# Side work of an attention-and-scan kernel: results taken one step later, with a third PSUM bank

## Chip, cores and metric

One core of a Trainium2 chip. The metric is the time on the device in microseconds (us); of several runs the median counts.

## What is computed

The input x holds 16 images of 256 channels by 1024 positions, in fp32. Two layers follow each other, each added to x:

- Layer 0: a group norm (16 groups), then a transformer block: layer norm, attention with four heads of 32 over the 1024 positions, projection, a second layer norm, a feed-forward pair of matrices with GELU.
- Layer 1: a second group norm, then a state-space layer. From the normed input come u and z (512 channels each), a gate, and from u the step sizes (softplus), B and C (64 states each). The heart is a recurrence along the 1024 positions:

```python
def step(h, inp):
    d_t, B_t, C_t, u_t = inp
    dA = jnp.exp(d_t[..., None] * A)
    h = dA * h + (d_t * u_t)[..., None] * B_t[:, None, :]
    y = jnp.einsum('bdn,bn->bd', h, C_t)
    return (h, y)
...
y = (ys + u * D) * silu(z)
out = (y @ out_proj_w.T) * sigmoid(gate)
```

It runs over 512 channels with 64 states each, so over 32768 rows of 1024 positions per image.

## The kernel before

**The main loop.** The recurrence is cut into units: one unit is 2 x 128 rows by 512 positions, so an image has 256 units and the run 4096. The list `units` (line 805) goes over image b, half t of the positions, channel block k, quarter q and i from 0 to 7. For each unit n the loop (lines 946 to 984) issues, in this order:

- `load(n + 6)`: SP loads a 512 KB tile dub (line 832), and at times the tiles bt, ct and pieces;
- `inputs(n + 4)`: POOL multiplies it with B (line 842);
- `scan(n, 0)` and `scan(n, 1)`: DVE runs the two recurrences (line 864);
- `decay(n + 2)`: PE makes the exponents (line 851) and ACT the exponentials (line 854), in four PSUM banks (pool `aps`), which come free with the scans;
- a piece of side work, if one is due;
- pieces of `outputs` (line 888): PE multiplies with C (lines 901 and 913), ACT copies out, SP stores ys. It takes a group of eight units at once, and its pieces on PE lie in the units i = 0 to 5 of the next group.

**The side work.** While image b is scanned, everything else is done beside it: `first_norm(b + 1)`, `gate_and_store(b - 1)`, `attention_layer(b + 1)` and `scan_inputs(b + 1)`, in this order (line 952). They are generators. Each `yield` gives a weight, and the loop takes the next step when enough has come due:

```python
rate, due = total / (UNITS - AHEAD - 3), 0.0
...
due += rate
while due > 0.0:
    due -= next(side, 1e9)
```

A step of weight 1 is thus about one unit, and two small steps can fall in the same unit. For image 0 the side work runs ahead of the loop, where nothing else runs; the last `gate_and_store` runs behind it.

**Order.** Lines 995 to 1005 hold PE, ACT, DVE and POOL to the order in which the code issues the instructions. SP's order is chosen by the scheduler. Each engine works through its own queue in order, so an instruction that waits holds up all behind it.

**PSUM.** There are eight banks: four of `aps`, one of `yps` (outputs), one of `accp` (the attention's sum of values, tag "av") and two of `mm`. In the loop all results of the side work are in the two banks of `mm` in turn, by `psum` (line 98).

**The places that the change touches:**

- `group_norm` (line 225): sums on DVE, means on PE (line 233), variance through Ln and Exp on ACT (lines 258, 259), then the multiplication on DVE (line 262). It runs in `first_norm` (tile gn) and in `scan_inputs` (tile xp).
- `layer_norm` (line 266): per half of the positions a mean on PE (line 270, ln_m), the subtraction on DVE (line 277), squares on ACT (line 279), the variance on PE (ln_v), Ln and Exp on ACT (lines 294, 296), the multiplication on DVE (line 301). It runs twice in `attention_layer`.
- z in `scan_inputs` (lines 567 to 588): eight products on PE (line 580), each with a tanh on ACT (line 585). `finish_z` multiplies on DVE (line 569) and stores (line 571) at the next step.
- Softplus (lines 684 to 736), for four channel blocks d: `begin` (PE, then absolute value and Exp on ACT), `more` (copy and relu on ACT, lines 694, 695), `rest` (two subtractions on DVE, lines 699, 700), then Ln and three splittings.
- Output product in `gate_and_store` (lines 783 to 799): four results in eight steps on PE (line 789); `finish` takes each on DVE (lines 776, 778) after the next product's first half. `come` holds loads that are issued step by step (line 309: ys, ud, zs, gs, xr, kept), before DVE uses them (lines 760, 764).
- `spread_c` (line 873): once per image POOL clears cd, a tile of 128 x 4096 (line 876), and for each half of the positions ACT writes C into a few of its places with eight copies (line 880).

Of the kernel before, what the change touches and what calls it, by code (L numbers as in the profile page):

```python
# [11 lines left out]
F32 = mybir.dt.float32  # L12
# [7 lines left out]
P = 128  # L20
# [3 lines left out]
HL = 512  # L24
# [9 lines left out]
TB = 512  # L34
# [18 lines left out]
def attention_then_scan_kernel(  # L53
# [44 lines left out]
    def psum(name, dims=P):  # L98
        src = mm if beside["scan"] else next(alone)
        return src.tile([P, HL], F32, name=name, tag="mm" if src is mm else "a")[:dims]  # L100

    def work(name, n=L):
        return wide.tile([P, L + 2 + CONV], F32, name=name, tag="wide")[:, :n]
# [4 lines left out]
    def hs(h):  # L108
        return ts(h, HL)
# [71 lines left out]
    for k in range(KC):  # L181
# [5 lines left out]
        nc.sync.dma_start(rel[ts(k, P), :], t)  # L187


    def weights(*specs):  # L190
# [34 lines left out]
    def group_norm(src, dst):  # L225
# [33 lines left out]
        nc.scalar.activation(v, v, AF.Exp, scale=-0.5)  # L259
        yield 1.5  # L260
        for k in range(KC):
# [4 lines left out]
    def layer_norm(src, dst, g, b):  # L266
        def mean_of(parts, name):
            m = psum(name)
            for k in range(KC):
                nc.tensor.matmul(m, avg, parts[k], start=(k == 0), stop=(k == KC - 1))  # L270
            return m
# [10 lines left out]

        m = mean_of([t[:, hs(0)] for t in src], "ln_m")
        yield 1
        q0 = centre(0, m)
        m = mean_of([t[:, hs(1)] for t in src], "ln_m")
        yield 1.2
        q1 = centre(1, m)
        vs = [mean_of(q0, "ln_v")]
        yield 1.2  # L290
        vs.append(mean_of(q1, "ln_v"))
        yield 1
        for v in vs:
            nc.scalar.activation(v, v, AF.Ln, bias=eps)
        for v in vs:
            nc.scalar.activation(v, v, AF.Exp, scale=-0.5)
        yield 2
        for h in range(2):
# [238 lines left out]
    def scan_inputs(b):  # L537
# [28 lines left out]

        def finish_z():
            for d, hf, z, t, ps in ready:
                nc.vector.scalar_tensor_tensor(z[:, hs(hf)], t, 1.0, ps, ALU.add, ALU.mult)
                if hf == 1:  # L570
                    nc.sync.dma_start(zs[ts(d, P), :], z)
            ready.clear()

        for d in range(ND):
            z = work("z")
            for hf in range(2):
                finish_z()
                ps = psum("z_ps")
                for k in range(KC):
# [124 lines left out]
        for d in range(ND):  # L704
            items = [more(d, *items[0]), begin(d, 1)]
            yield 1
            items[1] = more(d, *items[1])
            rest(*items[0])
            yield 1.4
            rest(*items[1])  # L710
# [32 lines left out]
    def gate_and_store(b):  # L743
# [39 lines left out]
        for o in range(KC):  # L783
            for hf in range(2):
                ps = psum("m_ps")
                for q in range(2):
                    first = o * HL + hf * 2 + q
                    for d in range(ND):
# [3 lines left out]
                        )  # L792
                    if q == 0:
                        finish()
# [77 lines left out]

    def spread_c(b, t):
        if t == 0:
            now["cd"] = hst.tile([P, TB // 16, P], F32, name="cd", tag="cd")
            nc.gpsimd.memset(now["cd"], 0.0)
        ct = blocks[b, t]["ct"].rearrange("p (a c e) -> p a c e", c=4, e=4)
        for c in range(4):
            for j in range(2):
                nc.scalar.activation(  # L880
                    now["cd"][:, :, 40 * c + j : 40 * c + j + 7 : 2], ct[:, :, c],
                    AF.Identity, scale=par[:, j : j + 1],
                )
# [4 lines left out]
    def outputs(b, t, k, q):  # L888
        if (k, q) == (0, 0):
            now["yb"] = yps.tile([P, HL], F32, name="yb", tag="yb")  # L890
            nc.vector.memset(now["yb"][:, 256:], 0.0)  # L891
        cd, yb, hbuf = now["cd"], now["yb"], now["h", q % 2]
        out4 = yb[:, 256:].rearrange("p (j a m e) -> p a e j m", a=2, j=2, e=4)
# [52 lines left out]
    for n, (b, t, k, q, i) in enumerate(units):  # L946
# [32 lines left out]
        if i == 0 and n > 0:  # L979
            g = outputs(*units[n - 1][:4])  # L980
            next(g)
            running.append(g)
        if (k, q, i) == (0, 0, 6):
            spread_c(b, t)
    for g in running:
# [75 lines left out]
```

## Time and profile before

| What | us |
|---|---|
| Median of three runs | 13823.3 (13804.61 to 13835.7) |
| Profiled execution, its own time | 13784.86 |
| Span of the profiled execution | 13782.7 |
| of it before the first scan | 392.8 |
| of it behind the last scan | 45.3 |
| VectorE busy | 12135.5 (88%) |
| TensorE busy | 11113.2 (81%) |
| GpSimd busy | 10477.2 (76%) |
| ScalarE busy | 8088.7 (59%) |
| Mean granted TensorE clock | 0.732 of full speed |

PE, DVE, ACT, POOL and SP are TensorE, VectorE, ScalarE, GpSimd and SyncE. A row of the costliest groups names line, engine, operation and tiles, how often it ran, then its busy time and the mean of one in ns, and behind the bar how long the engine stood idle just before and what ended that. The table of waits says the same per pair: who waited, for whom, how long in all, how often, and the longest. "issue" is idle time for which the profile shows no cause.

### The profile page before, as it was taken

Reading aid. Unit: us, or ns where it says so; the run is one execution under the profiler, and the core shown is the slowest. Engines: PE = TensorE matmul, PEld = TensorE weight load, DVE = VectorE, ACT = ScalarE, POOL = GpSimd, SP = SyncE. Lnnn points to the kernel's source line nnn. Section 1 sums busy time; section 2 is a strip of 40 time slices with the busy share of each in tenths; the row PEclk is TensorE's granted clock in tenths of the full one; section 3 lists DMA queues with packets and bytes.
Section 4 is the critical chain, followed back from the end, with each engine's and each line's share of the span. In section 5 each row is a group of like instructions: output and inputs, shape, how many; then the busy total and the mean of one; then the engine's idle time right before and its main releaser. Section 6 shows DMA issues by size and latency. Waiting matters only on the chain. (4 is left out here: it accounts for less than half of the span.)

```text
span 13782.7 us, 435036 instructions
## 1 busy us (share of the span) xinstructions
PE 11113.2 (81%) x185744; PEld 5728.7 (42%) x185744; DVE 12135.5 (88%) x11699; ACT 8088.7 (59%) x14245; POOL 10477.2 (76%) x8214
## 2 busy tenths in 40 slices
PE   7787878878787787978879788797887978878767
PEld 3344444444444444444444444444444444434434
DVE  3898898898898889888898888889888898888898
ACT  3666665656655565655656655566555655556644
POOL 0787777777787777777777787777777777777788
PEclk8686767867777686876767777677776776867767
DMA  1566566565665656556565565656656565565666
GB/s 55 196 207 230 187 214 208 201 222 196 211 207 199 218 201 223 194 199 218 197 231 186 197 226 191 232 185 202 219 191 230 187 214 205 194 228 187 209 219 223
DMA packets 964174, 2804.18 MB, mean 203 GB/s; under 512 B 138162, under 2 KB 285747, under 8 KB 962228
## 3 DMA queue, kind: packets, MB, share of 16 engines
q1 hardware_dynamic: 962228, 2776.34, 58.8%
q8 instruction: 1452, 23.79, 0.7%
q14 instruction: 494, 4.05, 0.1%
HBM read 2514.18 MB, written 261.62 MB: 201 GB/s over the span
## 5 line engine op out<-in xcount | busy, mean ns | idle before, releaser
L842 POOL TENSOR_TENSOR dub<-dub,bt 128x512 f32<-128x512 f32 x8192 | 10422.4, 1307 | 3254.5 <-DMA dub<-dus 2878.4
L854 ACT ACTIVATE a<-a,acol 128x512 f32<-128x512 f32 x8192 | 5064.9, 660 | 3728.2 <-PE a L851 3689.1
L864 DVE TENSOR_TENSOR_SCAN h<-a,last,dub 128x512 f32<-128x512 f32 x4096 | 4932.9, 1261 | 227.0 <-POOL dub L842 128.8
L864 DVE TENSOR_TENSOR_SCAN h<-a,dub 128x512 f32<-128x512 f32 x4096 | 4700.9, 1201 | 276.7 <-POOL dub L842 186.6
L851 PE MATMUL a<-pieces,pick 48*128 48x512 bf16 x8192 | 2914.9, 480 | 2103.1 <-DVE h L864 2037.8
L901 PEld LDWEIGHTS yb<-h,cd 128*32 128x32 f32 x131072 | 2677.2, 140 | 2166.2 <-issue 1847.3
L901 PE MATMUL yb<-h,cd 128*32 128x64 f32 x131072 | 3090.5, 265 | 160.9 <-DVE yb L891 115.9
L851 PEld LDWEIGHTS <-pick 48*128 48x128 bf16 x8192 | 498.0, 96 | 2507.4 <-issue 2293.2
L408 PE MATMUL s_ps<-ka,qa 32*128 32x512 f32 x2048 | 1115.7, 1009 | 23.2 <-DVE mx L399 15.2
L399 DVE TENSOR_REDUCE mx<-s_ps 128x1 f32<-128x512 f32 x1024 | 654.9, 678 | 279.0 <-PE s_ps L408 278.2
L913 PEld LDWEIGHTS yb<-turn,y 128*16 128x16 f32 x32768 | 418.9, 120 | 960.3 <-ACT y L909 484.6
L909 ACT COPY y<-yb 128x256 f32<-128x256 f32 x1024 | 383.4, 374 | 693.6 <-PE yb L901 688.3
L913 PE MATMUL yb<-turn,y 128*16 128x32 f32 x32768 | 555.2, 216 | 193.8 <-ACT y L909 173.0
L444 PE MATMUL st_ps<-qa,ka 33*128 33x512 f32 x2048 | 590.2, 613 | 25.9 <-ACT pt L452 25.5
L432 PE MATMUL av<-pt,vv 128*64 128x512 f32 x2048 | 572.7, 635 | 4.3 <-ACT sums L390 3.3
L452 ACT ACTIVATE pt<-st_ps 128x512 f32<-128x512 f32 x1024 | 558.9, 609 | 28.8 <-PE st_ps L444 28.4
L408 PEld LDWEIGHTS s_ps<-ka,qa 32*128 32x128 f32 x2048 | 345.4, 274 | 402.3 <-DVE mx L399 221.4
L630 PE MATMUL g_ps<-w,xp 128*128 128x256 f32 x1536 | 475.2, 468 | 0.0
L630 PEld LDWEIGHTS g_ps<-w,xp 128*128 128x128 f32 x1536 | 401.9, 329 | 137.6 <-issue 92.6
L789 PE MATMUL m_ps<-w,xs 128*128 128x256 f32 x1024 | 316.7, 459 | 10.9 <-DVE xs L764 10.9
L921 ACT COPY yo<-yb 128x256 f32<-128x256 f32 x512 | 193.1, 377 | 222.2 <-PE yb L913 219.7
L615 DVE SCALAR_TENSOR_TENSOR u<-up,cwh,u 128x1024 f32<-128x1024 f32 x192 | 300.9, 1567 | 23.8 <-ACT u L607 23.6
(135 smaller groups left out, 7593.8 us busy)
## 6 DMA issues: line engine op xcount, KB each, us to landing
dub<-dus SPq DMA_DIRECT2D x4096, 512.0 KB
dps<-pc SPq DMA_DIRECT2D x384, 128.0 KB
pieces<-dps SPq DMA_DIRECT2D x1024, 48.0 KB
xs<-in_x_dram SPq DMA_DIRECT2D x64, 512.0 KB
xs<-kept SPq DMA_DIRECT2D x64, 512.0 KB
zs<-z SPq DMA_DIRECT2D x64, 512.0 KB
ud<-u SPq DMA_DIRECT2D x64, 512.0 KB
dus<-du SPq DMA_DIRECT2D x64, 512.0 KB
```

The lines of the kernel that those rows point to most:

```text
L399: nc.vector.tensor_reduce(mx[:, e, c, hf : hf + 1], s, AX.X, ALU.max)
L408: nc.tensor.matmul(s, qa[r, ts(c, P)], ka[r, hs(hf)], start=True, stop=True)
L432: nc.tensor.matmul(av[ts(e, 2 * DH)], vv[j // (NJ // 2)][:, j % (NJ // 2), 2 * pair + e, :], pts[e], start=(j == 0), stop=(j == NJ - 1),)
L444: nc.tensor.matmul(s, ka[r, ts(j, P)], qa[r, hs(hf)], start=True, stop=True)
L452: nc.scalar.activation(pt, s, AF.Exp)
L630: nc.tensor.matmul(ps[:, ts(q, C)], xp[k][:, ds(first + t, P, 4)], wg_s[:, k, t, :], start=(i == 0), stop=False,)
L842: nc.gpsimd.tensor_tensor(v, v, blocks[b, t]["bt"], ALU.mult)
L851: nc.tensor.matmul(a, w, pieces[r], start=True, stop=True)
L854: nc.scalar.activation(a, a, AF.Exp, scale=acol[:, at : at + 1])
L864: nc.vector.tensor_tensor_scan(now["h", q % 2][:, 2 * i + e, :], decays[n][e], loaded[n][:, e, :], first, ALU.mult, ALU.add,)
L901: nc.tensor.matmul(yb[ts(g, 32), ts(s, 64)], cd[:, at // 16, ts(c, 32)], hbuf[:, :, at : at + 4], start=(c == 0), stop=(c == 3),)
L913: nc.tensor.matmul(out4[32 * s : 32 * s + 16, half, e], y2[:, 64 * s + e : 64 * s + 64 : 4], turn[:, e], start=True, stop=True,)
```

## The change

- A new `psum3` hands out the two banks of `mm` and the one of `accp` in turn. It serves ln_m, ln_v, z_ps and m_ps.
- `group_norm`: one more step boundary between Exp and the multiplication (weights 1.2 and 1 for 1.5).
- `layer_norm`: both mean products are issued ahead of the first subtraction, the first variance product ahead of the second subtraction; a further step boundary before the multiplication (1.3 and 1 for 2).
- z: a result is taken when two are outstanding, so one step later.
- Softplus: `begin` of the second half goes one step behind `more` of the first, beside the first half's `rest`.
- Output product: a result is taken after the next product's second half.
- cd is made and cleared once, ahead of the loop; the eight copies of `spread_c` are issued in two groups of four at i = 5 and 6, where all eight were at i = 6.

```diff
@@ -98,6 +98,13 @@
     def psum(name, dims=P):
         src = mm if beside["scan"] else next(alone)
         return src.tile([P, HL], F32, name=name, tag="mm" if src is mm else "a")[:dims]
+
+
+    three = cycle((mm, mm, accp))
+
+    def psum3(name):
+        src = next(three) if beside["scan"] else next(alone)
+        return src.tile([P, HL], F32, name=name, tag={mm: "mm", accp: "av"}.get(src, "a"))
 
     def work(name, n=L):
         return wide.tile([P, L + 2 + CONV], F32, name=name, tag="wide")[:, :n]
@@ -186,6 +193,9 @@
         nc.vector.tensor_tensor(t, t, rw, ALU.add)
         nc.sync.dma_start(rel[ts(k, P), :], t)
 
+    cd = hst.tile([P, TB // 16, P], F32, name="cd", tag="cd")
+    nc.gpsimd.memset(cd, 0.0)
+
 
     def weights(*specs):
         w = wts.tile([P, 4672], F32, name="w", tag="w")
@@ -257,7 +267,8 @@
         yield 1.2
         nc.scalar.activation(v, v, AF.Ln, bias=eps, scale=per)
         nc.scalar.activation(v, v, AF.Exp, scale=-0.5)
-        yield 1.5
+        yield 1.2
+        yield 1
         for k in range(KC):
             nc.vector.tensor_tensor(grouped(dst[k]), grouped(dst[k]), over_group(v), ALU.mult)
             yield 1.2
@@ -265,7 +276,7 @@
 
     def layer_norm(src, dst, g, b):
         def mean_of(parts, name):
-            m = psum(name)
+            m = psum3(name)
             for k in range(KC):
                 nc.tensor.matmul(m, avg, parts[k], start=(k == 0), stop=(k == KC - 1))
             return m
@@ -280,21 +291,23 @@
                 qs.append(q)
             return qs
 
-        m = mean_of([t[:, hs(0)] for t in src], "ln_m")
-        yield 1
-        q0 = centre(0, m)
-        m = mean_of([t[:, hs(1)] for t in src], "ln_m")
+        m0 = mean_of([t[:, hs(0)] for t in src], "ln_m")
+        yield 0.7
+        m1 = mean_of([t[:, hs(1)] for t in src], "ln_m")
+        yield 0.7
+        q0 = centre(0, m0)
         yield 1.2
-        q1 = centre(1, m)
         vs = [mean_of(q0, "ln_v")]
+        q1 = centre(1, m1)
         yield 1.2
         vs.append(mean_of(q1, "ln_v"))
-        yield 1
+        yield 0.8
         for v in vs:
             nc.scalar.activation(v, v, AF.Ln, bias=eps)
         for v in vs:
             nc.scalar.activation(v, v, AF.Exp, scale=-0.5)
-        yield 2
+        yield 1.3
+        yield 1
         for h in range(2):
             for k in range(KC):
                 d = dst[k][:, hs(h)]
@@ -564,18 +577,18 @@
         zs = dram.tile([DI, L], F32, name="zs", tag="zs")
         ready = []
 
-        def finish_z():
-            for d, hf, z, t, ps in ready:
+        def finish_z(keep=0):
+            while len(ready) > keep:
+                d, hf, z, t, ps = ready.pop(0)
                 nc.vector.scalar_tensor_tensor(z[:, hs(hf)], t, 1.0, ps, ALU.add, ALU.mult)
                 if hf == 1:
                     nc.sync.dma_start(zs[ts(d, P), :], z)
-            ready.clear()
 
         for d in range(ND):
             z = work("z")
             for hf in range(2):
-                finish_z()
-                ps = psum("z_ps")
+                finish_z(1)
+                ps = psum3("z_ps")
                 for k in range(KC):
                     nc.tensor.matmul(
                         ps, win_s[:, k, ds(DI + d * P, P)], body[k][:, hs(hf)],
@@ -702,11 +715,13 @@
         items = [begin(0, 0)]
         yield 1
         for d in range(ND):
-            items = [more(d, *items[0]), begin(d, 1)]
-            yield 1
+            items[0] = more(d, *items[0])
+            yield 0.8
+            items.append(begin(d, 1))
+            rest(*items[0])
+            yield 1.3
             items[1] = more(d, *items[1])
-            rest(*items[0])
-            yield 1.4
+            yield 0.8
             rest(*items[1])
             for ps, e, s in items:
                 nc.scalar.activation(s, s, AF.Ln)
@@ -782,7 +797,7 @@
 
         for o in range(KC):
             for hf in range(2):
-                ps = psum("m_ps")
+                ps = psum3("m_ps")
                 for q in range(2):
                     first = o * HL + hf * 2 + q
                     for d in range(ND):
@@ -790,7 +805,7 @@
                             ps[:, ts(q, C)], us[d][:, ds(first, P, 4)], wo_s[:, d, :],
                             start=(d == 0), stop=(d == ND - 1),
                         )
-                    if q == 0:
+                    if q == 1:
                         finish()
                     if come:
                         come.pop(0)()
@@ -870,15 +885,12 @@
 
 
 
-    def spread_c(b, t):
-        if t == 0:
-            now["cd"] = hst.tile([P, TB // 16, P], F32, name="cd", tag="cd")
-            nc.gpsimd.memset(now["cd"], 0.0)
+    def spread_c(b, t, some):
         ct = blocks[b, t]["ct"].rearrange("p (a c e) -> p a c e", c=4, e=4)
-        for c in range(4):
+        for c in some:
             for j in range(2):
                 nc.scalar.activation(
-                    now["cd"][:, :, 40 * c + j : 40 * c + j + 7 : 2], ct[:, :, c],
+                    cd[:, :, 40 * c + j : 40 * c + j + 7 : 2], ct[:, :, c],
                     AF.Identity, scale=par[:, j : j + 1],
                 )
 
@@ -889,7 +901,7 @@
         if (k, q) == (0, 0):
             now["yb"] = yps.tile([P, HL], F32, name="yb", tag="yb")
             nc.vector.memset(now["yb"][:, 256:], 0.0)
-        cd, yb, hbuf = now["cd"], now["yb"], now["h", q % 2]
+        yb, hbuf = now["yb"], now["h", q % 2]
         out4 = yb[:, 256:].rearrange("p (j a m e) -> p a e j m", a=2, j=2, e=4)
         if t == 0:
             nc.scalar.copy(now["last"][:, ds(64 * k + 16 * q, 16)], hbuf[:, :, TB - 1])
@@ -980,8 +992,8 @@
             g = outputs(*units[n - 1][:4])
             next(g)
             running.append(g)
-        if (k, q, i) == (0, 0, 6):
-            spread_c(b, t)
+        if (k, q) == (0, 0) and i in (5, 6):
+            spread_c(b, t, ((0, 1), (2, 3))[i - 5])
     for g in running:
         for _ in g:
             pass
```

## The prediction

> **What bounds the kernel now.** I read the page's busy times first, then who VectorE (DVE) waited for over the whole run, then one wait in order of time, then two stretches by engine. "Unit" is one pass of the main loop (two scans), "step" one piece of side work between two yields. The lines of the page:
>
> ```profile
> PE 11113.2 (81%) x185744; PEld 5728.7 (42%) x185744; DVE 12135.5 (88%) x11699; ACT 8088.7 (59%) x14245; POOL 10477.2 (76%) x8214
> ...
> L842 POOL TENSOR_TENSOR dub<-dub,bt 128x512 f32<-128x512 f32 x8192 | 10422.4, 1307 | 3254.5 <-DMA dub<-dus 2878.4
> ```
>
> DVE is the fullest engine: 12135.5 of 13782.7 us. Its two scan groups (L864, 4932.9 and 4700.9 us) make up most of it, about 2.35 us a unit. DVE stands idle for 1647 us, and only that can be won, since the change takes no work from DVE. POOL needs 2 x 1.307 = 2.6 us a unit, against 13344.6/4096 = 3.26 us that a unit takes on average, so it is not the bound as a whole. The waits of DVE (total, times, longest):
>
> ```profile
> DVE h L864 <- POOL dub L842: 315.5, 287, 9.9
> ...
> DVE z L569 <- ACT z_t L585: 117.8, 93, 3.0
> DVE d_ps L699 <- ACT d_ps L695: 111.3, 97, 22.6
> DVE xn L301 <- ACT ln_v L296: 105.0, 32, 5.1
> DVE gn L262 <- ACT gn_v_ps L259: 103.8, 16, 8.4
> DVE xn L277 <- PE ln_m L270: 89.0, 32, 9.5
> DVE m_ps L776 <- PE m_ps L789: 81.3, 60, 4.7
> ...
> DVE xp L262 <- ACT gn_v_ps L259: 43.2, 16, 3.8
> ```
>
> Seven of these are waits for a result that was asked for one or two steps earlier, and they are what the change moves. The same answer for the stretch before the loop (to 392.8 us), for image 0 and for the last 722 us lets me take those out. For images 1 to 14 the remainder per image is: z 104.3/14 = 7.45, d_ps 5.0, ln_v 6.4, first group norm (gn) 7.2, ln_m 4.9, m_ps 4.9, second group norm (xp) 2.6; together 38.5 us of an image's 845. One of them in order of time (start, length, engine, what):
>
> ```profile
> 1221.65 3.52 POOL L876 MEMSET cd<- 128x4096 f32 x1
> ...
> 1225.20 2.44 ACT L880 ACTIVATE cd<-ct,par 128x128 f32<-128x128 f32 x8 [3.73 <-POOL cd L876]
> ...
> 1227.55 1.20 ACT L854 ACTIVATE a<-a,acol 128x512 f32<-128x512 f32 x2
> 1228.76 1.28 ACT L258 ACT_TABLE_LOAD   x1
> ...
> 1231.81 1.22 DVE L262 TENSOR_TENSOR gn<-gn,gn_v_ps 128x1024 f32<-128x1024 f32 x1 [6.68 <-ACT gn_v_ps L259]
> ```
>
> ACT takes its queue in order: it stands 3.7 us for POOL's memset, does C's tile, the exponentials, two table loads, and DVE waits 6.7 us for that. Two stretches of image 5 (length, PE, PEld, DVE, ACT, POOL busy): the output product and the z product:
>
> ```profile
> 4665.50:4696.20 30.70, 28.61 (x434) 22.05 (x434) 25.66 (x27) 12.14 (x22) 22.56 (x19) 0.92 0.71 255
> 5136.20:5168.20 32.00, 29.38 (x371) 12.82 (x370) 24.24 (x27) 16.31 (x29) 16.59 (x15) 0.87 0.56 185
> ```
>
> Here PE is busy for 28.61 of 30.7 and 29.38 of 32.0 us. If DVE stops waiting for a result in them, PE is next.
>
> **What the Trainium skill says.** "Perfetto Trace Analysis", Optimizing Tensor Performance, says that independent matmul groups should rotate through PSUM banks so that evacuation overlaps the next matmuls. Here PE's waits hold no entry for a z or output bank; DVE does the waiting. The third bank only makes room to take a result later. "ScalarE: Activation LUTs", What ACT_TABLE_LOAD costs, gives about 1283 ns a load and 1380 ns of draining. The load agrees (1.28 us); the drain does not show, the next activation starts at 1230.05, when the load ends. "TensorE: Matmul & The Clock Gate", What's actually happening, says that the clock is throttled by default and activity releases it. The trace fits: 0.50 in the stretch of the group-norm stall (4597.2 to 4607.5 us, PE busy 1.74 of 10.3), and the four z matmuls take 3.78 us cold and 1.98 warm. Shorter stalls may thus help PE; I price that at nothing.
>
> **The change part by part, for one of images 1 to 14.** The order of both programs' instructions (without times) tells in which unit each step falls; images 1 to 14 all have the same order. No instruction of PE, DVE or ACT is added or removed, nor a table load. POOL loses 15 of 16 memsets; the one that stays (3.5 us) lies before the loop, where POOL is busy 15.5 of 392.8 us.
>
> *First group norm and C's tile.* ACT's 3.7 us wait goes. C's eight copies (2.44 us) are split over two units, with ACT busy for some 3 of the 3.4 us of each. Ln and Exp stay in unit 8, the multiply moves from unit 9 to 10, so DVE reaches it 2.35 us later. 3.7 + 2.35 + 1.2 (half the copies, done a unit sooner) covers 7.2. Gain 7.2, at least 6.5. What hides the chain is the scan pair of the extra unit; without it some 2.3 us would come back. Behind the memset on POOL stood the inputs for four units ahead; they come 3.5 us sooner, and DVE was not waiting for them there.
>
> *Second group norm.* From Ln/Exp to multiply it was one unit and is two. 2.6 is about one scan pair of 2.35 and the step's own lag. Gain 2.6.
>
> *Layer norms, means.* In the second norm both mean products and the first subtraction fell in the same unit (DVE waits 4.1); now they are in units 144, 145 and 146. Gain 4.1. In the first norm mean and subtraction stay one unit apart, and the second mean only moves to the first one's unit: the 0.8 stays. Range 2 to 4.9: that unit has 5.4 us of mean products on PE at the cold clock, with the next exponents' products queued behind.
>
> *Layer norms, variance.* The first norm's multiply goes from one unit after Ln/Exp to two: 4.0 becomes 1.65, gain 2.35. The second was two units apart and remains so (148 to 150): its 2.4 stays. Range -0.6 (Ln now shares the unit of the second variance product, and waits for it) to 4.8. Gain 2.35.
>
> *z product.* Each result is taken a step later, but the last two still one unit after their tanh, with both products in one unit. The waits on z (7.45) would mostly go. PE allows 32.0 - 29.38 = 2.6, and it may run perhaps 1 us late into the next units before DVE needs its exponents. Gain 3.5; range 2.6 to 7.45 (all, if PE turns warm sooner).
>
> *Output product.* Same reasoning: 30.70 - 28.61 = 2.1 of 4.9; the means of the layer norm follow at once on PE, so nothing is lent. Gain 2.0; range 0 to 4.9.
>
> *Softplus.* Subtraction and relu of the first half stay one unit apart for three of four d; for the first d they now fall in the same unit, which costs one scan pair, 2.35. For the second half the later product takes the two 0.65 us waits away. Net -1.1; range -3 to +2. Queued behind this new DVE wait are the second subtraction and the next unit's scans, and behind those PE's exponent products.
>
> *SP's queue.* SP issues every load and store in order. In the new order the loads of ys, ud and zs come 1 to 4 units later, and DVE's first use of ud one unit later; the first wait (2.4 us, L760) should go, two later uses lose a unit and may each wait about 0.9. I take 0; range -2.5 to +2. The two kept stores stand together and hold the next dub load about one unit longer; POOL is four units ahead, which hides it.
>
> Sum: 7.2 + 2.6 + 4.1 + 2.35 + 3.5 + 2.0 - 1.1 + 0 = 20.65 us an image, x14 = 289; image 0 gives some 3 more (its second group norm), image 15 and the ends nothing. That is 292 us. The profiled execution took 13784.9 us (span 13782.7): 13493 by this sum. It lies 38.4 us below the median of the runs, 13823.3; from there the forecast is 13823 - 292 = 13531 us, -2.1%. The low ends sum to 6.5 + 2.6 + 2 - 0.6 + 2.6 + 0 - 3 - 2.5 = 7.6 an image, 13717 us; the high ends to 7.2 + 2.6 + 4.9 + 4.8 + 7.45 + 4.9 + 2 + 2 = 35.85, 13321 us.
>
> **The rivals.** *All seven waits vanish.* For it: the clock may rise with fewer gaps, and PE's busy time is modelled. Against it: PE's share in the two stretches above. 38.5 x 14 = 540 us: 13283 us. *Only the group norms pay*, and what the layer norms and products save turns into waits for PE or ACT: 9.8 x 14 + 3 = 140 us, 13683 us. For it: several distances between step and use don't grow in the new order. Against it: the second norm's means clearly do. *Slower: the load queue.* Twelve stores an image (2 kept, 4 zs, 4 ud, 2 out) wait in SP's queue for side results, and dub loads queue behind each. If taking results later made each cost DVE one scan pair, 12 x 2.35 = 28.2 against 20.65 won: 7.5 x 14 = 106 us, 13929 us. It decides from the point where a load slips by more than the two units between its issue and POOL's use; POOL's 2878 us of waiting for those loads speaks for it. Against it: DVE's waits for POOL lie mainly in attention, where DVE has no side work, and not at stores.
>
> **How the numbers follow.** Sum as forecast, 13440 to 13610: 0.55. All waits or nearly so (13270 to 13440): 0.17. Group norms alone (13610 to 13780): 0.20. Load queue, slower: 0.04. Effects cancel, within 0.2%: 0.04. 0.2% (28 us) is about what a measurement of this kernel can tell from no change. Faster is 0.55 + 0.17 + 0.20 = 0.92. The range 13340 to 13730 leaves out some two fifths of the second case, under a third of the third and all of the last two: 0.07 + 0.06 + 0.08, about 0.2.
>
> **What would show it.** First group norm's wait on ACT gone (L262's 103.8 us near zero) and no MEMSET in the loop; ln_m near 25 us and ln_v near 70 in total; z and m_ps falling by more than half, while DVE's waits "issue" or POOL before scans rise by some 50 us in the product stretches; d_ps not falling. It would be wrong if d_ps or L760 waits grow by more than 5 us an image, or if L864's wait for POOL (315.5 us) rises by over 100 us, which would mean the load queue.

## The result and the profile after

| What | before | after |
|---|---|---|
| Median of four runs, us | 13815.9 (13804.61 to 13835.7) | 13727.7 (13706.4 to 13736.77) |
| Profiled execution: span, us | 13782.7 | 13704.6 |
| VectorE busy, us | 12135.5 | 12201.4 |
| VectorE idle (span less busy), us | 1647.2 | 1503.2 |
| Mean length of images 1 to 14, us | 847.3 | 839.7 |

(A fourth run of the kernel before stands beside the three of the first table.) The ratio is 0.9932, 95% interval 0.9915 to 0.995: 88 us faster, where 292 were forecast. The last row of the table is the distance between the first scans of successive images in the trace. It fell by 7.6 us, not 20.65. That is 107 us for 14 images; image 0 took 12 us longer (805.1 and 817.3), and the stretch before the loop 20 us longer. In the profiled executions of this study that stretch took either 393 to 395 us or 410 to 416, and parts of the change stand in both groups (before 392.9, after 413.2), so I don't count these 20 us as the change's.

The page of the changed kernel, busy time by engine:

```profile
PE 11070.1 (81%) x185744; PEld 5715.5 (42%) x185744; DVE 12201.4 (89%) x11699; ACT 8077.5 (59%) x14245; POOL 10432.3 (76%) x8199
```

The count of DVE's instructions is the same (x11699), its busy time is 66 us more. The waits of DVE (total us, times, longest):

```profile
DVE h L879 <- POOL dub L857: 359.1, 331, 3.5
DVE mx L412 <- PE s_ps L421: 317.2, 249, 56.7
DVE d_ps L712 <- ACT d_ps L708: 182.3, 128, 22.6
DVE h L879 <- issue: 173.9, 246, 3.0
DVE xs L775 <- DMA xs<-ud: 68.3, 32, 6.8
DVE xn L314 <- ACT ln_v L308: 65.6, 31, 5.1
...
DVE z L583 <- ACT z_t L598: 35.6, 53, 3.1
DVE m_ps L791 <- PE m_ps L804: 27.2, 18, 4.7
DVE xn L288 <- PE ln_m L281: 24.5, 9, 9.4
...
DVE xp L273 <- ACT gn_v_ps L269: 9.5, 16, 3.8
DVE gn L273 <- ACT gn_v_ps L269: 6.2, 16, 2.5
```

Every wait that was to go went: gn 103.8 to 6.2, xp 43.2 to 9.5, ln_m 89.0 to 24.5, ln_v 105.0 to 65.6, z 117.8 to 35.6, m_ps 81.3 to 27.2, together 371 us. But idle time as a whole fell by 144 only (d_ps rose by 71, the scans' waits for POOL by 44, s_ps by 39, of which 11 lie ahead of the loop, and the gate's for ud by 22), and 66 of that went into busy time. Where does an instruction take longer? The addition of tok and gn that follows the first group norm (L328 before, L341 after; the profile calls tok xs). Both its operands lie in SBUF. First the kernel before, image 6 (counted from 0), DVE by start and length:

```profile
5453.93 1.22 DVE L262 TENSOR_TENSOR gn<-gn,gn_v_ps 128x1024 f32<-128x1024 f32 x1 [7.29 <-ACT gn_v_ps L259]
...
5460.94 1.20 DVE L328 TENSOR_TENSOR xs<-xs,gn 128x1024 f32<-128x1024 f32 x1
```

and POOL there:

```profile
5447.24 12.30 POOL L842 TENSOR_TENSOR dub<-dub,bt 128x512 f32<-128x512 f32 x10
5461.78 2.70 POOL L842 TENSOR_TENSOR dub<-dub,bt 128x512 f32<-128x512 f32 x2 [2.24 <-DMA dub<-dus]
```

Then the same place after the change, DVE:

```profile
5461.56 1.20 DVE L273 TENSOR_TENSOR gn<-gn,gn_v_ps 128x1024 f32<-128x1024 f32 x1
5462.68 2.33 DVE L879 TENSOR_TENSOR_SCAN h<-a,dub 128x512 f32<-128x512 f32 x2
5464.92 8.61 DVE L341 TENSOR_TENSOR xs<-xs,gn 128x1024 f32<-128x1024 f32 x1
5473.45 2.32 DVE L879 TENSOR_TENSOR_SCAN h<-a,dub 128x512 f32<-128x512 f32 x2
5475.70 1.19 DVE L341 TENSOR_TENSOR xs<-xs,gn 128x1024 f32<-128x1024 f32 x1
```

and POOL:

```profile
5447.92 24.53 POOL L857 TENSOR_TENSOR dub<-dub,bt 128x512 f32<-128x512 f32 x20
```

Before, POOL was out of loaded inputs at 5459.54 and had paused for 1.4 us when the addition began: 1.20 us. After, it multiplies without a pause from 5411.11 until 5472.45, and the addition comes in the 44th of these multiplications; it lasts 8.61 us and ends 1.08 us after the last, about its own length. The next addition, with POOL idle, takes 1.19 us. The multiplication with gn_v_ps and the scans, which read one operand from PSUM, take 1.2 us each all along. In the whole run it is one row (total us, mean ns), before and after:

```profile
L328 DVE TENSOR_TENSOR xs<-xs,gn 128x1024 f32<-128x1024 f32 x32 | 40.7, 1273 | 0.0
```

```profile
L341 DVE TENSOR_TENSOR xs<-xs,gn 128x1024 f32<-128x1024 f32 x32 | 117.8, 3685 | 0.0
```

77 us, more than DVE's whole extra busy time. That led to theory 1: POOL's unbroken multiplications keep the addition out. The stall that the change removed had been POOL's time to work off its backlog. The experiments below call what they test against it a rival, or theory 2 and rival 3; each says what it means.

### The profile page after: what moved, and what is told of

Same layout as the page of the kernel before. It is cut to its first block, busy times and chain, and to the rows that moved or that the text cites. A ratio compares the mean times of both kernels' runs of the same rounds, so it can differ in the third digit from the quotient of the medians.

```text
span 13704.6 us, 434983 instructions
## 1 busy us (share of the span) xinstructions
PE 11070.1 (81%) x185744; PEld 5715.5 (42%) x185744; DVE 12201.4 (89%) x11699; ACT 8077.5 (59%) x14245; POOL 10432.3 (76%) x8199
## 5 line engine op out<-in xcount | busy, mean ns | idle before, releaser
L804 PEld LDWEIGHTS m_ps<-w,xs 128*128 128x128 f32 x1024 | 261.2, 328 | 77.1 <-issue 49.5
```

Source lines behind the costliest of these rows:

```text
L804: nc.tensor.matmul(ps[:, ts(q, C)], us[d][:, ds(first, P, 4)], wo_s[:, d, :], start=(d == 0), stop=(d == ND - 1),)
```

## The experiments

Times are medians, ratios are to runs of the kernel before that were made beside them. The median of the kernel before lay between 13811.6 and 13822.5 us in six such sets, so the difference of two medians from different sets is uncertain by some 10 us for that alone. The "ledger" is the prediction's sum, part by part. "Image" is the mean length of images 1 to 14 in the trace (before 847.3, after 839.7 us); code is cut to the lines that matter.

### Each part alone

**gn_only**: the kernel before, with

```diff
-            nc.gpsimd.memset(now["cd"], 0.0)
+    nc.gpsimd.memset(cd, 0.0)
...
-        if (k, q, i) == (0, 0, 6):
-            spread_c(b, t)
+        if (k, q) == (0, 0) and i in (5, 6):
+            spread_c(b, t, ((0, 1), (2, 3))[i - 5])
...
-        yield 1.5
+        yield 1.2
+        yield 1
```

> One part of the change alone, on the kernel before: C's tile cleared once, its copies split over two units, and the group norm's multiply one unit later. The ledger of the prediction: both waits of the group norms on ACT go and nothing replaces them, 9.8 us an image, 140 us, ratio about 0.990. Theory 1 (VectorE's addition of tok and gn is starved while POOL multiplies without a pause): the wait on ACT goes as well, but the addition after it, 1.2 us so far in the middle of its times, takes about 8 us in most images, so that the net gain is 2 to 5 us an image, 30 to 70 us, ratio 0.995 to 0.998. Theory 2 (the late loads of the gate are what costs, whatever the addition does): the addition stays near 1.2 us and the waits of the gate for ud grow.

Measured: 13812.9 us, ratio 0.9994 (0.9985 to 1.0002), image 848.6. Waits gn and xp fell to 6.2 and 8.2 us, and nothing was gained:

```profile
L332 DVE TENSOR_TENSOR xs<-xs,gn 128x1024 f32<-128x1024 f32 x32 | 129.5, 4050 | 0.0
```

The addition took 89 us more; m_ps rose from 81.3 to 122.1 us and the scans' waits for POOL from 315.5 to 352.1. The ledger's 140 us are refuted, and less is left than theory 1 had it (30 to 70 us). Of the 11.1 us an image that are missing (9.8 forecast, 1.3 lost) the additions took 6.3; DVE's busy time as a whole grew by 5.2. m_ps and the scans' waits for POOL, 2.9 and 2.6, are the next, and other entries fell.

**psum_only**: the kernel before, with `psum3` for z and m_ps and both results taken a product later.

```diff
-                finish_z()
-                ps = psum("z_ps")
+                finish_z(1)
+                ps = psum3("z_ps")
...
-                ps = psum("m_ps")
+                ps = psum3("m_ps")
...
-                    if q == 0:
+                    if q == 1:
```

> Another part alone, on the kernel before: the third PSUM bank, with the z and output products' results taken one product later; norms, C's tile and softplus as before. The ledger gives 3.5 + 2.0 = 5.5 us an image, about 77 us, ratio about 0.9945. If PE bounds these stretches more tightly than I read, the waits on z_ps and m_ps go and waits before the scans for POOL or without a visible cause take their place: under 2 us an image, ratio 0.998 or more. The addition of tok and gn should stay near 1.2 us, since the group norm still stalls ahead of it.

Measured: 13684.4 us, ratio 0.9903 (0.9888 to 0.9918), image 838.75: 8.6 us an image, above the ledger's 5.5.

```profile
DVE z L576 <- ACT z_t L591: 38.1, 48, 3.0
...
DVE m_ps L782 <- PE m_ps L795: 27.5, 18, 4.7
```

Units 168 to 191 (z) took 6.4 us less (89.7 to 83.3), units 16 to 31 (output) 1.5 less, as a mean of images 1 to 14. In image 5, units 168 to 183, before and then psum_only (length, PE, PEld, DVE, ACT and POOL busy, clock, DMA share, GB/s):

```profile
5120.27:5180.83 60.56, 49.17 (x719) 22.89 (x719) 51.47 (x49) 30.00 (x52) 43.53 (x33) 0.80 0.53 181
```

```profile
5120.46:5175.07 54.61, 47.36 (x719) 22.70 (x719) 49.61 (x48) 29.66 (x52) 40.13 (x32) 0.79 0.61 202
```

I had taken the densest 32 us of this stretch as PE's bound. Over the whole of it PE had 11.4 us to spare, and 6 of them were won. In the output stretch it was not PE that came next either: in image 5 its units 16 to 31 lose the 4.1 us of waits on m_ps, and the scans then wait 3.0 us for POOL, which waits for its loads; PE is busy for 39.7 of 50.4 us. In images 1 to 14 these waits for POOL are 37 us, where the kernel before has none in this stretch.

**ln_only**: the kernel before, with the layer norm's new order and `psum3` in it.

> The layer norm's new order alone (with the third bank for its means and variances), on the kernel before. The ledger gives 4.1 + 2.35 = 6.45 us an image, 90 us, ratio about 0.9935. If the parts add up, the runs so far leave for it 0.68 - 0.97 - 0.06 + 0.50 = 0.15%, about 20 us, ratio 0.998 to 0.999: then the one unit by which it delays all later steps costs elsewhere what it saves at ln_m and ln_v.

Measured: 13728.3 us, ratio 0.9932 (0.9919 to 0.9945), image 840.7: 6.65 us an image, where the ledger had 6.45. My second guess, from what the other parts left, missed, because parts don't add up.

```profile
DVE xn L309 <- ACT ln_v L303: 75.1, 32, 5.1
...
DVE xn L283 <- PE ln_m L276: 25.8, 11, 9.6
...
DVE xp L268 <- ACT gn_v_ps L265: 10.5, 16, 3.8
```

ln_m and ln_v together fell by 93 us. The last line was not foreseen: the second group norm's wait went from 43.2 to 10.5 us without any edit to that norm. So the ledger counted those 2.6 us an image for the group norm's step, and the layer norm's part already takes them.

**softplus_old**: the changed kernel with

```diff
-            items[0] = more(d, *items[0])
-            yield 0.8
-            items.append(begin(d, 1))
-            rest(*items[0])
-            yield 1.3
+            items = [more(d, *items[0]), begin(d, 1)]
+            yield 1
             items[1] = more(d, *items[1])
-            yield 0.8
+            rest(*items[0])
+            yield 1.4
```

> The changed kernel with the softplus put back to its old order. If the new order costs what the waits on d_ps suggest (5.0 us an image before, 9.7 after), this is 4 to 5 us an image faster than the changed kernel: about 60 us, ratio to the kernel before 0.988 to 0.990, and the d_ps waits total near 111 us. Rival: what is saved there turns up again as waits before the scans (PE's exponents), and the time stays within 15 us of the changed kernel's 13728, ratio 0.993.

Measured: 13652.1 us, ratio 0.9881 (0.9864 to 0.9897), image 837.0. The time fell as expected; the d_ps waits went only from 182.3 to 147.1 us, not to 111. The new softplus costs 2.5 us an image in that wait, 2.7 in the image, 5.4 by the medians (76 us over 14 images). The changed kernel's profiled execution was 21 us under its median, which makes some of the gap between the last two; the rest is open, so the cost is 2.7 to 5.4.

### The parts together

**psum_ln** is psum_only with the layer norm's part; **psum_ln_cd** has C's tile split too.

> The kernel before with the third bank for z, output and layer norm and the layer norm's new order; group norm, C's tile and softplus as before. If parts add up with what is measured so far: 0.97 + 0.15%, ratio 0.988 to 0.990, and faster than the changed kernel by 0.4%. By the ledger: 5.5 + 6.45 us an image, 167 us, ratio 0.988. If the steps' places decide (all later steps shifted by one unit), anything from 0.985 to 0.993.

> The same with C's tile cleared once and its copies split over two units; the group norm keeps its old distance, so no step moves. Ledger: ACT's 3.7 us wait for POOL's memset lies on the group norm's chain, so 3.7 us an image less, 52 us, 0.38% under its neighbour without this edit. Theory 1 (POOL works off a backlog there, and the stall of VectorE is what lets it run dry): the stall on ACT falls from 6.7 to about 3 us, the addition of tok and gn goes up by about as much, and the time stays within 0.1% of its neighbour.

Measured: 13631.8 us, 0.9862 (0.9844 to 0.988), image 835.7; then 13607.2 us, 0.9844 (0.9831 to 0.9858), image 833.4. The edit to C's tile took gn's wait from 105.6 to 41.1 us; 2.3 us of 4.6 an image arrived, between my two figures. DVE still waits 2.5 us an image there, and the addition stays short:

```profile
L339 DVE TENSOR_TENSOR xs<-xs,gn 128x1024 f32<-128x1024 f32 x32 | 44.8, 1403 | 0.0
```

softplus_old is psum_ln_cd with the group norm's extra step in both norms. So that step costs 13652 - 13607 = 45 us, 3.6 us an image (additions 81 us more, gn 35 and xp 2 less: 44), and the ladder of the change is, in us an image: third bank and layer norm -11.7, C's tile -2.3, group norm's step +3.6, softplus +2.7, together -7.6 (each number is rounded).

### Is it POOL that holds the addition up?

**breaks**: the changed kernel, with a clear of 128 numbers ahead of POOL's multiplications.

```diff
+            if 10 <= n % UNITS < 30:
+                nc.gpsimd.memset(gap, 0.0)
             nc.gpsimd.tensor_tensor(v, v, blocks[b, t]["bt"], ALU.mult)
```

> The changed kernel with a clear of 128 numbers on POOL ahead of each of its multiplications in units 10 to 29 of an image, which leaves pauses between two multiplications. Theory 1 (the addition of tok and gn is starved as long as POOL's multiplications follow each other without a pause): the addition falls from 5 to 9.5 us in most images to 1.3 to 2.4, the gate's waits for ud fall with it, and the time falls by 5 to 7 us an image, 70 to 100 us under the changed kernel, ratio to the kernel before about 0.986 to 0.988. Rival: the addition is slow for another reason (its inputs, or ACT), it stays at 5 us or more, and the time stays at 0.993 or above.

Measured: 13739.0 us, ratio 0.9936 (0.9919 to 0.9954). The additions took 146.5 us. Theory 1's forecast failed, but the trace shows no pause either: the clears overlap the multiplications, which follow each other every 1.26 us (1.22 without), and a long addition still ends 1.1 us after POOL has run dry (image 6). Inconclusive.

**pool_add**: softplus_old with the addition on POOL in the loop; **cd_pool**: the same edit on psum_ln_cd.

```diff
-            nc.vector.tensor_tensor(tok[k], tok[k], gn[k], ALU.add)
+            adder = nc.gpsimd if beside["scan"] else nc.vector
+            adder.tensor_tensor(tok[k], tok[k], gn[k], ALU.add)
```

> The changed kernel with the old order of softplus, and in the main loop the addition of tok and gn is made by POOL instead of VectorE, so that VectorE has no such addition that could be starved. Theory 1: VectorE's busy time falls by the 120 us that these additions take in the kernel without this edit, and the time by 5 to 9 us an image, 70 to 120 us: 13530 to 13580, ratio 0.979 to 0.983. Rival (POOL has a backlog there, and VectorE must wait for POOL by one way or the other): the scans' waits for POOL rise by 100 us, also because POOL has 2.6 us more to do for each addition, and the time stays within 25 us of 13652, ratio 0.987 to 0.990.

> The same kernel of ratio 0.9844, with the addition of tok and gn made by POOL in the main loop. There it takes VectorE 45 us in total and is not starved, so the gain should be those 42 us at most, less what VectorE then waits for POOL: 13565 to 13600, ratio 0.982 to 0.984. If, by the rival, POOL is the bound of that stretch, nothing is gained, since each addition costs POOL about 2.6 us: 13600 to 13630.

Measured: pool_add 13599.3 us, 0.9843 (0.9829 to 0.9856), 53 us under softplus_old and between the two forecasts; cd_pool 13609.5 us, 0.9842 (0.9827 to 0.9857), nothing gained on psum_ln_cd. Moving a starved addition away pays; moving one that isn't starved doesn't. In pool_add the gate now waits for dub's loads, 73.7 us, where it had been 11.6.

**late_add**: softplus_old with four empty steps ahead of the additions.

> The changed kernel with the old order of softplus (ratio 0.9881, its additions of tok and gn take 126 us in total), and four empty steps ahead of these additions. Theory 1 says that an addition gets nothing as long as POOL multiplies without a pause; POOL is working off its backlog and should have pauses again four units later, so that the first addition falls from 8 to 9 us to 1.2 to 2.4 us in most images, and the time by some 5 us an image, less what four more shifted steps cost: 13580 to 13640. Rival: the addition is slow wherever it stands (over 5 us in most images), and the time is not under 13640.

Measured: 13633.3 us, 0.9864 (0.9849 to 0.9879). The additions fell from 125.9 to 58.3 us; two still took over 7 us. But in image 3, DVE and then POOL:

```profile
2943.41 1.23 DVE L343 TENSOR_TENSOR xs<-xs,gn 128x1024 f32<-128x1024 f32 x1
```

```profile
2939.85 13.02 POOL L857 TENSOR_TENSOR dub<-dub,bt 128x512 f32<-128x512 f32 x9 [0.68 <-DMA dub<-dus]
```

Here POOL shows no pause from 2939.85 on, and the addition got in: POOL's nine multiplications took 13.02 us instead of some 11. So "no pause, no entry" is too strong; entry at the boundary of two multiplications exists. It came in the third multiplication behind a pause of 0.68 us, though; the one that was kept out in the changed kernel came in the 44th.

**pool_stop**: softplus_old with one copy of 128 numbers on POOL that waits for the first addition.

```diff
             nc.vector.tensor_tensor(tok[k], tok[k], gn[k], ALU.add)
+            if beside["scan"] and k == 0:
+                nc.gpsimd.tensor_copy(stop, tok[k][:, :1])
```

> The changed kernel with the old order of softplus (ratio 0.9881), and one copy of 128 numbers on POOL that reads the result of the first addition of tok and gn. It stands in POOL's queue behind the multiplications of unit 15; so far POOL went on to the last one loaded, of unit 17, while the addition of unit 11 waited. Theory 1 (POOL's unbroken multiplications keep the addition out, and it goes on when POOL stops): POOL stops four multiplications, 4.9 us, earlier, and additions of 8.2 to 9.4 us fall to 3.3 to 4.5; over the 14 images 45 to 55 us less of VectorE's busy time, and the time 20 to 50 us less: 13600 to 13630. Rival: the addition's length has nothing to do with where POOL stops; it stays at 8 to 9 us, and POOL's stop adds to it.

(`stop` is a tile of 128 x 1.) Measured: 13578.4 us, ratio 0.9824 (0.9804 to 0.9844), 74 us under softplus_old (by the trace 55 us in images 1 to 14). POOL in image 6, then the addition's row:

```profile
5379.75 13.57 POOL L858 TENSOR_TENSOR dub<-dub,bt 128x512 f32<-128x512 f32 x11
5394.50 0.18 POOL L344 COPY stop<-xs 128x1 f32<-128x1 f32 x1 [1.19 <-DVE xs L342]
5394.64 5.92 POOL L858 TENSOR_TENSOR dub<-dub,bt 128x512 f32<-128x512 f32 x4
```

```profile
L342 DVE TENSOR_TENSOR xs<-xs,gn 128x1024 f32<-128x1024 f32 x32 | 45.3, 1418 | 0.0
```

The first addition starts at 5393.24, as POOL ends unit 15, and takes 1.20 us; POOL stands 1.19 us for it. The only edit is a wait on POOL, and DVE's addition falls from 125.9 to 45.3 us, further than I expected: POOL is just coming to its stop when the addition starts. Here too that is POOL's 44th multiplication without a pause. This shows theory 1's cause: it is POOL's going on that keeps the addition out.

What late_add left open can be counted in the traces of all 18 kernels. I take the additions of tok and gn that begin while POOL multiplies and goes on without a pause. All 63 that began within POOL's first nine instructions since its last pause took at most 2.31 us. Of the 68 that began in the 33rd or later, 67 took 3.6 to 9.7 us. So an addition is kept out when POOL has gone without a pause for long, and gets in at the next boundary when POOL paused shortly before. The same holds for all DVE instructions of the side work that take two operands of 128x1024 from SBUF: none of 4015 took over 2.5 us when it began within POOL's first 13 instructions, 9 of 315 did from the 14th to the 32nd, and 134 of 140 after that. Whether the length of the run itself decides, or the loaded inputs that have piled up for POOL, these traces don't separate.

### What the shifted steps do

All four build on psum_ln_cd (13607 us). **shift_after** has an empty step behind the first norm's addition. **first_only** and **second_only** have the group norm's extra step in one norm only. **second_after** has that step behind the second norm's multiplications.

> The kernel with the third bank, the layer norm's new order and C's tile split (ratio 0.9844), with one empty step more just after the first norm's additions of tok and gn: the group norm and the addition stay where they were, every later step comes a unit later, as in the changed kernel. The group norm's extra step in both norms makes 0.9881 of that 0.9844. Theory 1 (that loss is the starved addition): the addition stays near 1.3 us and the time within 15 us of 13607. Rival 3 (what costs is that all later steps fall in other units, beside other loads and other outputs): 13640 to 13660, ratio near 0.988, with the waits m_ps and u up by some 20 and 15 us.

> The kernel with the third bank, the layer norm's new order and C's tile split (13607 us, ratio 0.9844), with the group norm's extra step in the first norm only. With it in both norms 13652, in the second only 13534. If the two steps add up, the first costs 118 us and gives 13725 here, ratio 0.993. Theory 1 alone (starved additions, some 80 us, against 2.5 us an image of waits on ACT that vanish): plus 45 us, 13652. If the place of all later steps decides (an empty step after the addition made 13644): anything from 13610 to 13730, but the additions take 80 us more in every case.

> The same kernel of ratio 0.9844, with the group norm's extra step in the second norm only. The layer norm's new order has already taken that norm's wait from 43 to 10.5 us, so that by theory 1 there is nothing left to gain or to lose: within 15 us of 13607. By rival 3, a shift of the steps after attention's start costs here too: over 20 us more.

> The same kernel of 13607 us, with the extra step of the second norm put after its multiplications instead of ahead of them. With it ahead of them the time was 13534, far more than the 3 us of waits it removed. If the place of the later steps did that, it does it here too: within 20 us of 13534, with the scans' waits for POOL near 290 us instead of 382. If it was the norm's own distance: near 13607.

| Kernel | us | ratio (95%) | image, us | additions, us | scans' waits for POOL, us | xp, us |
|---|---|---|---|---|---|---|
| psum_ln_cd | 13607.2 | 0.9844 (0.9831 to 0.9858) | 833.4 | 44.8 | 382.2 | 10.5 |
| shift_after | 13644.3 | 0.9876 (0.9858 to 0.9894) | 836.1 | 44.1 | 362.4 | 40.9 |
| first_only | 13691.3 | 0.991 (0.9893 to 0.9927) | 838.9 | 133.1 | 345.5 | 40.9 |
| second_only | 13534.2 | 0.9795 (0.9777 to 0.9812) | 828.6 | 43.9 | 293.5 | 7.8 |
| second_after | 13560.7 | 0.9817 (0.9797 to 0.9837) | 829.1 | 44.3 | 277.8 | 40.8 |

Two lines of second_only that stand behind the table:

```profile
DVE h L877 <- POOL dub L855: 293.5, 284, 3.7
...
DVE xp L273 <- ACT gn_v_ps L268: 7.8, 15, 3.8
```

Against psum_ln_cd the first norm's step costs 84 us. The entries that it was to move give 88 more of additions, 30 of xp's wait and 35 less of gn's, together 83; others move too (z 33 more, the scans for POOL 37 less, s_ps 30 less, and DVE's busy time as a whole grows by 37 only), so the match is no proof. An empty step behind the addition costs 37, where theory 1 had at most 15: rival 3 is right as well. xp's wait is 30 us longer there: whether the second norm must wait for ACT depends on where its steps fall, and this shift undoes what the layer norm's part had given it. The second norm's step wins 73 us, against both expectations. Of these, 47 come as well when the step stands behind the norm's multiplications (by the images 60 of 68), although xp's wait is then 30 us longer; so most of the gain goes with the place of the steps behind that norm, and the scans' waits for POOL fall from 382 to 278 and 294 us with it. Which loads or products meet better there I have not settled. Nor do the two steps add up: +84 and -73 alone, +45 together. second_only beats both kernels.

### The same at a second place

**tail_stop**: second_only, and in the last image POOL copies one column of each gate addition's result.

```diff
             nc.vector.scalar_tensor_tensor(us[d], us[d], col("D", d), ys[d], ALU.mult, ALU.add)
+            if b == B - 2:
+                nc.gpsimd.tensor_copy(stop, us[d][:, :1])
```

> The kernel with the extra step in the second norm only (13534 us, ratio 0.9795), and in the last image four copies of 128 numbers on POOL, each reading the result of a gate's addition of us and ys. These four additions take 14 to 17 us each beside POOL's multiplications in all kernels so far, 60 us together, the kernel before included. Theory 1: with the copy POOL stops four units after the scan before the addition instead of six, at most 4.9 us earlier each, 20 us in all, or up to 50 us if POOL comes to its stop as early as it did at the addition of tok and gn: 13485 to 13515. If they are slow for another reason, they stay at 14 us and the time within 15 us of 13534.

Measured: 13501.0 us, ratio 0.9769 (0.9752 to 0.9785), 33 us under second_only; the two ratios' intervals overlap. In the traces the scans of the last image take 16 us less (672.9 to 656.8). The four additions took 17.0, 16.0, 14.8 and 14.8 us and now 9.7, 8.1, 5.1 and 5.8; two of the products behind them, which also take two SBUF operands, now take 11.4 where they took 1.5 and 2.1. The last addition in second_only, then in tail_stop:

```profile
13165.08 14.81 DVE L773 SCALAR_TENSOR_TENSOR xs<-xs,vec 128x1024 f32<-128x1024 f32 x1
```

```profile
13153.04 5.78 DVE L774 SCALAR_TENSOR_TENSOR xs<-xs,vec 128x1024 f32<-128x1024 f32 x1
```

Stopping POOL earlier shortens the addition here too. The kernel before already has this: its four additions there take 14.0 to 16.0 us, so some of what DVE counts as busy was never work. This is the fastest version found.

## Why the prediction was wrong

The direction was right; the gain was under a third of the forecast. That the median still lies within the range of 13340 to 13730, 2 us from its end, is luck: it reached that far for the case that only the group norms pay, which is not what happened.

The step that failed is the first of the ledger: that the group norms' waits on ACT, once gone, are won, with nothing behind them getting slower. It rests on the sentence "only that can be won, since the change takes no work from DVE", which takes busy time for fixed. It grew by 66 us with the same instructions. Of the 13.0 us an image that are missing (20.65 less 7.6), the ladder puts 11.1 on the group norms and C's tile, 1.6 on softplus and 0.3 on the rest. By the prediction's own steps, in us an image:

- **First and second group norm, C's tile (gain 7.2 + 2.6): failed.** Measured alone: +1.3 (gn_only). The waits did go. My sentence "behind the memset on POOL stood the inputs for four units ahead; they come 3.5 us sooner, and DVE was not waiting for them there" looked for what POOL's freedom could give, and not for what a POOL that never runs dry does to the next DVE instruction with two SBUF operands. The term left out was the addition behind the norm: 77 us in the changed kernel, 5.5 an image. Another 2.6 were counted twice, since the layer norm's part takes xp's wait too (ln_only). The rest of the 11.1, some 3, is near the 44 us by which the scans' waits for POOL grew; why they grew was not tested. It is the first norm's step that costs; the second's pays (second_only), but not by the wait that the ledger named. "SBUF — State Buffer", SBUF: two separate sides, of the Trainium skill says that VectorE and GpSimd share a port pair as an exclusive lock, held for a whole instruction, when the VectorE instruction has two SBUF inputs and GpSimd's reads SBUF. I did not use it. The trace agrees on the blocking, and goes further: as I read that page the loser waits for one instruction, here 1.3 us, but the addition stood out for six multiplications (8.61 us). C's tile alone, with the other parts in, gave 2.3 of its 3.7.
- **Layer norms (4.1 + 2.35): right**, 6.65 measured alone, and ln_m and ln_v fell by as much in ln_only (93 us). xp's 33 us, which were not forecast, came on top in the list of waits and did not arrive in the time.
- **z (3.5) and output (2.0): the waits went, but the bound named behind them was wrong.** 6.4 and 1.5 in their units, 8.6 for the image. PE's bound in a window of 32 us was no bound for 60 us, so z was too small; in the output stretch POOL's loads came next and not PE, so that the size there was right by chance. With the layer norm's part, 3.6 of the sum of both (15.25) are lost; the two together still give 11.7 against the ledger's 11.95.
- **Softplus (-1.1): sign right, size -2.7** by the images, near the end of its range. The wait grows by 2.5 an image against the old order in the same kernel.
- **SP's queue (0): -2.7** at the gate in the changed kernel (22 us for ud, 15.5 for dub). psum_ln_cd shows 69.5 us there too, so the group norm is not its only cause; this was not tested further.
- **Rivals.** "Only the group norms pay" gave 13683, near the measured 13728 and for the wrong reason: the group norms paid nothing, the rest paid. The slower load queue did not come: scans' waits for POOL rose by 44 us, not 100.
- **What would show it.** The signs of the forecast came (gn, no clear in the loop, ln_m 24.5, ln_v 65.6, z and m_ps; the scans' waits in the output stretch rose by 39 us), with less than a third of the gain. They were signs in the list of waits. Of the counter-signs one came, narrowly: d_ps grew by 71 us, 5.1 an image. A sign on DVE's busy time was missing, and there the step failed.

What the additions cost, some two fifths of the miss in the changed kernel and about half of it in gn_only, is shown by pool_stop (one wait on POOL returns 74 us). Open remain why the scans wait longer for POOL in gn_only and in the changed kernel, why the place of the steps behind the second norm alone gives 47 us (second_after), and what it is in POOL's long runs that keeps an addition out.

## What to carry to other kernels

Before a stall is removed, look at what the other engines do with it: here POOL caught up in it, and the next VectorE instruction with two SBUF operands needed a pause of POOL. Set busy time beside the list of waits, with minimum and maximum of each instruction, since the time in which such an instruction is kept out is counted as busy (8.61 us for an addition of 1.2). And where work is spread by weights, an added step moves everything behind it; try the parts alone and the steps one by one: the best version here keeps one of the two added steps and the old softplus.

## What the hardware showed that I had not expected

- A VectorE addition of two SBUF operands (128x1024, fp32) beside POOL's multiplications of two SBUF operands took 1.2 us alone, up to 2.3 us when it got in at the next boundary of two multiplications (the one behind it then took 2.25 us instead of 1.26), and 3.6 to 9.7 us at the first norm when it didn't. A scalar_tensor_tensor of the same size took 13 to 17 us at the last image's gate. Which of the two happens goes with how long POOL has gone without a pause: none of 4015 was kept out within its first 13 instructions since a pause, 134 of 140 from the 33rd on.
- The scans beside the same multiplications stayed at 1.2 us; they read one operand (a) from PSUM.
- A clear of 128 numbers between two of POOL's multiplications did not help (146.5 us for the additions, against 117.8 without); a wait of POOL for the addition's result did (45.3 against 125.9).
